# A planner-ordered graph-network stack: a 14th tile buffer, small softmax steps moved between engines, and the gate's difference by VectorE from PSUM

## The chip, the cores and the metric

The kernel runs on one core of one Trainium2 chip. The metric is the device time of one execution in microseconds (us). All arithmetic is float32.

## The reference

`x` is 64 graphs of 256 nodes with 128 features, and `adj` is one 256 x 256 matrix for all graphs. Four layers follow each other. Each normalises `x`, applies ReLU, runs a graph operator and adds its result to `x`.

```python
def layer0(h):                                   # gated recurrent unit, five steps
    for _ in range(5):
        m = einsum('nm,bmd->bnd', adj, h)        # m_in and m_out are the same
        av = concatenate([m, m]); u3 = h @ u3_w.T + u3_b
        z = sigmoid(av @ w3_w.T + w3_b + u3)
        r = sigmoid(av @ w4_w.T + w4_b + u3)
        hv = tanh(av @ w5_w.T + w5_b + (r * h @ u5_w.T + u5_b))
        h = (1 - z) * h + z * hv
    return h
def layer1(h):                                   # h, h@A and 2(h@A)@A - h, then Theta1, bias, relu
def layer2(h):                                   # (adj@h + h) @ weight + bias, each row over its norm
def layer3(x):                                   # pairwise attention; W is adj here
    pre = s1[:, :, None, :] + s2[:, None, :, :] + b_lin     # 256 x 256 x 256 for each graph
    e = einsum('bije,e->bij', where(pre >= 0, pre, 0.2 * pre), a) + adj
    return sigmoid(einsum('bij,bjf->bif', softmax(e, axis=2), x))
h = maximum(layernorm(x), 0); x = x + layerK(h)  # for K = 0, 1, 2, 3
```

Nearly all work is in `pre` of layer 3: 64 x 256 x 256 x 256 values of a sum, a kink and a weighted sum.

## The kernel before

The graphs are taken in 32 pairs. For each pair there are three kinds of work.

The **front** (`front`) does layers 0 to 2 and the projections of layer 3. It is one chain of about a hundred steps that hop between TensorE (PE), VectorE (DVE), ScalarE (ACT) and GpSimd (POOL). The first pair is done as two single graphs (`alone`). In each of the five steps of the recurrent unit ACT takes the tanh of the candidate out of a PSUM bank into `d` (L601), POOL subtracts the old state (`d - hT`, L605), and DVE multiplies by the gate (L608) and adds the state (L612). `norm` gives mean and variance by DVE (L463), then POOL the inverse root (`inverse_root`, L391 and L392), then DVE the product of minus mean and inverse root (L469), and then ACT applies both (L473).

The **tiles** are the body of layer 3. The kink is rewritten as a minimum (or a ReLU) of a column of `s1` and a row of `s2`, with the 256 hidden features in two halves of 128 partitions. A slot is four rows of two graphs, so one half of a slot is a tile of 128 x 2048 values. There are 2048 slots, so 4096 tiles. DVE makes tiles of the first half (L934, one instruction), ACT of the second (L946, eight), and POOL of either (L951, eight). PE scores a tile with four matmuls that sum over the features (`score`, L1010) into the score bank of that half of the pair. In a **joined** slot (a share of `SHARE`, here 3 in 10) DVE and POOL make one half each, an accumulating DMA that POOL issues (`add_pair`, L971) adds one tile to the other, and PE scores the sum once. The tiles lie in 13 SBUF buffers (`tiles`); a buffer is taken from the start of its making until PE has read it, or until the DMA has read it.

The **tail** (`tail`), twice in each pair, is the softmax and what follows: DVE adds a rank-one term to the scores (L806), POOL adds the broadcast rows `lin` (L818), DVE takes the row maximum (L822), ACT the exponential (L826), PE transposes and multiplies with `h3`, DVE takes the reciprocal (L846), ACT the tanh (L851), and POOL halves, adds 0.5 and adds the residual `x3` (L856, L857; in the very last tail these and the addition of `lin` are DVE's).

The order is written out ahead of time. A planner in the kernel keeps a clock for each engine, with a fixed cost for each operation (`ran`), and gives each engine in turn what is ready: steps of tails first, then steps of fronts (which may not run ahead of an even pace, `SPREAD`), then tiles. Tiles go to whichever of DVE, ACT and POOL is free. Each engine's instructions stay in that order on the chip (`in_order`); semaphores make them wait where the chip differs from the plan. SP's queue issues plain transfers: the inputs, `row` and `rows` (L745, L749) and the results (L860).

Of the kernel before, what the change touches and what calls it, by code (L numbers as in the profile page):

```python
# [21 lines left out]
MOST_POSITIVE = -MOST_NEGATIVE  # L22
PE, DVE, ACT, POOL = ENGINES = (mybir.EngineType.PE, mybir.EngineType.DVE, mybir.EngineType.Activation, mybir.EngineType.Pool)
SLOTS = 64
SHARE = (3, 10)
AHEAD_OF = 2
LOW = 1
ISSUE, ADDED, LANDED, SLACK = 0.65, 5.3, 6.6, 0.3

# [2 lines left out]
def kernel(  # L32
# [62 lines left out]
    banks = [psum.tile([P, NB * N], F32, name=f"bank{k}") for k in range(8)]  # L95


    clock = dict.fromkeys((PE, DVE, ACT, POOL), 0.0)
    queue = [0.0]
    SEEN = {PE: 0.25, DVE: 0.14, ACT: 0.18, POOL: 0.13}  # L100
# [21 lines left out]
    def by_feature(b, nb=NB):  # L122
        return b[:, 0:nb * N].rearrange("p (b n) -> p b n", b=nb)
# [31 lines left out]

    ident = const.tile([P, P], F32, name="ident")
    make_identity(nc, ident)
    place = work.tile([P, N], mybir.dt.int32, name="place", bufs=1)
# [19 lines left out]
    th_raw = const.tile([P, 5, D], F32, name="th_raw")  # L178
# [24 lines left out]
    gate_b = const.tile([P, 3], F32, name="gate_b")  # L203
    bz, br, bh = gate_b[:, 0:1], gate_b[:, 1:2], gate_b[:, 2:3]
    th = th_raw[:, 0:3, :]
# [9 lines left out]
    def first_constants():  # L215

        for c in range(NC):
            yield PE, 6.0, 1
            b = take()
            for k in range(NC):  # L220
                nc.tensor.transpose(b[0][:, k * P:(k + 1) * P], adj_n[:, k, c * P:(c + 1) * P], ident)
            t = ran(PE, 0.4, 6.0, b[1])
            yield DVE, t
            nc.vector.tensor_copy(adj_t[:, c, :], b[0][:, 0:N])
            t = ran(DVE, 0.35, t)
            spare.append([b[0], t])
# [28 lines left out]
        nc.vector.tensor_scalar(gate_b[:, 0:2], gate_b[:, 0:2], 0.5, None, op0=OP.mult)  # L255
        ran(DVE, 0.3)
        SET_UP.add("first")

# [196 lines left out]
    def norm(src, since, h):  # L455

        nb = src.shape[1]
        stats = work.tile([P, nb * NC, 3], F32, name="stats", bufs=4)
        mv = work.tile([P, nb * NC, 2], F32, name="mv", bufs=4)
        s, h = rows_of(src), rows_of(h)[:, :, 0:D]  # L460
        yield DVE, since
        for k in range(0, nb * NC, 2):
            nc.vector.bn_stats(stats[:, k:k + 2, :].rearrange("p k s -> p (k s)"), s[:, k:k + 2, :].rearrange("p k d -> p d k"))  # L463
        t = ran(DVE, STATS[nb], since)
        yield POOL, t
        inverse_root(mv[:, :, 1], stats[:, :, 2], 1.0 / D, OP.mult, LN_EPS, OP.add)
        t = ran(POOL, 1.45, t)
        yield DVE, t
        nc.vector.scalar_tensor_tensor(mv[:, :, 0], stats[:, :, 1], -1.0, mv[:, :, 1], op0=OP.mult, op1=OP.mult)  # L469
        t = ran(DVE, 0.1, t)  # L470
        yield ACT, t
        for k in range(nb * NC):
            nc.scalar.activation(h[:, k, :], s[:, k, :], AF.Relu, bias=mv[:, k, 0:1], scale=mv[:, k, 1:2])  # L473
        return ran(ACT, NORMED[nb], t)
# [5 lines left out]
    def front(p, batches):  # L480
# [31 lines left out]
        def seen(b):  # L512
            return by_feature(b[0], nb)
# [22 lines left out]
        for step in range(STEPS):  # L536
# [61 lines left out]
                t = ran(DVE, ELEMENTS[nb], t)  # L598
                spare.append([pv[0], t])
            else:  # L600
                nc.scalar.activation(d, seen(pv), AF.Tanh, bias=bh, scale=1.0)  # L601
                t = ran(ACT, TANH[nb], t)
                spare.append([pv[0], t])
                yield POOL, t
                nc.gpsimd.tensor_sub(d, d, hT)  # L605
                t = ran(POOL, 1.3, t)
            yield DVE, max(t, t_z)
            nc.vector.scalar_tensor_tensor(seen(pr), seen(pr), 1.0, d, op0=OP.add, op1=OP.mult)  # L608
            t = ran(DVE, ELEMENTS[nb], t, t_z)
            yield DVE, t  # L610
            hT_new = feature("hT", bufs=4)
            nc.vector.scalar_tensor_tensor(hT_new, seen(pr), 0.5, hT, op0=OP.mult, op1=OP.add)  # L612
            hT = hT_new
            t_hT = ran(DVE, ELEMENTS[nb])
            spare.append([pr[0], t_hT])
# [78 lines left out]
        t = ran(POOL, 1.35, t)  # L694

        yield DVE, t, 0, lambda: p < 2 or (p - 2, NC - 1) in TAILED
        x3 = kept("x3", [NC, D])
# [7 lines left out]
        h3 = kept("h3", [NC, D + 1])  # L705
        nc.gpsimd.memset(h3[:, :, :, D:D + 1], 2.0)
        t = yield from norm(x3, t, h3)
        yield PE, t, 1
        b = take()
        to_feature(b[0], h3)  # L710
        t = ran(PE, TURN[nb], t, b[1])
        yield ACT, t
        hT = kept("hT3", [N])
        nc.scalar.copy(hT, seen(b))
        t_hT = ran(ACT, COPY[nb], t)
        spare.append([b[0], t_hT])
        yield PE, t_hT, 1
        s2a = take()
        project(s2a[0], w2n[:, 0:P], hT)
# [13 lines left out]
        quarter = work.tile([P, P], F32, name="quarter", bufs=2)  # L733
# [4 lines left out]
        turned = work.tile([P, P], F32, name="turned", bufs=2)  # L738
        nc.vector.transpose(turned[:, 0:cols], quarter[:, 0:cols])
        s1o = kept("s1o", [NC])  # L740
        nc.vector.tensor_scalar(s1o.rearrange("p b c -> p (b c)"), turned[:, 2:cols:32], b_odd, None, op0=OP.add)
        ran(DVE, 0.65, t)
        row = dram.tile([2, NB * N], F32, name="row", bufs=4)
        for k in range(2):
            nc.sync.dma_start(row[k, 0:nb * N].rearrange("(q g i) -> g q i", g=4, i=32),  # L745
# [53 lines left out]
    def tail(u, pe, since):  # L799
# [3 lines left out]
        yield DVE, max(since, ops["t_lin"])  # L803
        sc = feat("sc", **SHORT)
        for k, (b, c) in enumerate(across(u)):
            nc.vector.scalar_tensor_tensor(sc[:, k, :], ops["s2o"][:, b, :], ops["s1o"][:, b, c:c + 1], pe[k], op0=OP.min, op1=OP.add)  # L806
        t = ran(DVE, 0.8, since, ops["t_lin"])
        used = banks_of.pop(u)
        spare.append([used, t])
        end = u == (NPAIR - 1, NC - 1)  # L810
        more = lin.to_broadcast([P, NB, N]) if ops["alone"] else lin
        if end:
            yield DVE, max(t, ops["t_lin"])
            nc.vector.tensor_add(sc, sc, more)
            t = ran(DVE, ELEMENTS[2], t, ops["t_lin"])
        else:
            yield POOL, max(t, ops["t_lin"])
            nc.gpsimd.tensor_add(sc, sc, more)  # L818
            t = ran(POOL, 1.3, t, ops["t_lin"])
        yield DVE, t  # L820
        nmx = work.tile([P, NB], F32, name="nmx")
        nc.vector.tensor_reduce(nmx, sc, AX.X, OP.max, negate=True)  # L822
# [40 lines left out]


    NSLOT = NPAIR * SLOTS
    tiles = [[relu_pool.tile([P, 4, NB, N], F32, name=f"rl{k}", bufs=1), 0.0] for k in range(13)]
    MOST = {DVE: 8, ACT: 3, POOL: 4}
    held = dict.fromkeys(MOST, 0)
    begun = {}
# [149 lines left out]


    CHAINS = {}
    STEPS_OF_FRONT, SPREAD, AHEAD = 109, 1.7, 2
    begun_fronts = [0]

    def begin(key, steps):
# [107 lines left out]
```

## Time and profile before

The median of three runs is 4924.24 us (4917.3 to 4930.92). The profiled execution took 4930.46 us, of which 4928.2 are the span from the first to the last instruction.

| engine | busy us | share of the span | its largest group | us of it |
|---|---|---|---|---|
| PE | 4768.4 | 97% | scoring, L1010 | 2211.3 and 1321.9 |
| DVE | 4713.3 | 96% | tiles, L934, 1817 of them | 4064.2 |
| POOL | 4670.5 | 95% | tiles, L951, 8144 instructions | 2966.0 and 874.8 |
| ACT | 4643.9 | 94% | tiles, L946, 10088 instructions | 4047.8 |
| DMA | | | joining, L971, 614 transfers of 1024 KB | 65.3% of 16 engines' span |

A group's line has the source line, the engine, the operation, its output and inputs by name, the shape and the count; behind the first bar stand the busy time of the group and the mean duration of one in ns; behind the second stand the engine's idle time just before these instructions and what ended it. Instructions of one engine overlap a little, so busy time over count can be less than the mean duration. A line of the view of waits has who waited for whom, the total in us, how often, and the longest.

### The profile page before, as it was taken

How to read it: one execution, taken by the hardware profiler on the slowest of the kernel's cores; microseconds unless marked ns; L12 is line 12 of the kernel's file. 1: busy time of each engine (PE TensorE's matmuls, PEld its weight loads, DVE VectorE, ACT ScalarE, POOL GpSimd, SP SyncE). 2: the span in 40 equal slices, each digit the busy share in tenths (PEclk: the TensorE clock that was granted, in tenths of full speed). 3: DMA queues.
4: the chain of work that ended last, by engine and by line, in shares of the span. 5: the costliest groups of instructions: out<-in, count | busy, mean ns of one | idle time of the engine just before them, and what ended most of it. 6: DMA issues, size and time to landing. Idle time of an engine off the chain costs nothing.

```text
span 4928.2 us, 134012 instructions
## 1 busy us (share of the span) xinstructions
PE 4768.4 (97%) x52471; PEld 1739.2 (35%) x52471; DVE 4713.3 (96%) x3389; ACT 4643.9 (94%) x12142; POOL 4670.5 (95%) x9473
## 2 busy tenths in 40 slices
PE   9999999999999999999999999999999999999987
PEld 4333333333333333333333333333333333333322
DVE  5999999999999999999999999999999999999998
ACT  6999999999999989999999999999999999999998
POOL 3999999999999999999999999999999999999997
PEclk9999999999999999999999999999999999999999
DMA  1666766767767666776776666777767767767677
GB/s 40 137 141 132 151 138 132 148 136 146 144 134 149 138 141 138 143 147 134 145 152 137 142 140 138 148 143 143 144 130 147 148 139 144 144 137 143 143 155 148
DMA packets 133540, 687.45 MB, mean 139 GB/s; under 512 B 15144, under 2 KB 50344, under 8 KB 54312
## 3 DMA queue, kind: packets, MB, share of 16 engines
q0 software_dynamic: 88416, 643.86, 65.3%
q1 hardware_dynamic: 43768, 35.01, 2.3%
q8 instruction: 410, 6.72, 0.5%
q14 instruction: 226, 1.85, 0.1%
q10 hardware_dynamic: 720, 0.00, 0.0%
HBM read 26.48 MB, written 8.52 MB: 7 GB/s over the span
## 4 chain that ended last, share of the span: by engine, by line
PE 31%; POOL 18%; DVE 12%; DMA 7%; ACT 6%; issue 4%; POOLq 0%; ACTq 0%; DVEq 0%
PE bank L1010 19%; POOL rl L951 14%; PE bank L397 11%; DVE rl L934 10%; DMA rl<-rl 7%; ACT rl L946 5%; POOL rl L971 2%; POOL d L605 1%; PE bank L428 1%; POOL mv L392 1%; DVE mv L469 0%; DVE hT L612 0%; PE bank L420 0%; DVE bank L608 0%; POOL sc L818 0%
## 5 line engine op out<-in xcount | busy, mean ns | idle before, releaser
L934 DVE TENSOR_TENSOR rl<-s1a,bank 128x2048 f32<-128x2048 f32 x1817 | 4064.2, 2277 | 100.3 <-DMA rl<-rl 59.2
L946 ACT ACTIVATE rl<-bank,s1b 128x256 f32<-128x256 f32 x10088 | 4047.8, 819 | 113.6 <-DMA rl<-rl 62.8
L951 POOL TENSOR_SCALAR rl<-s2n,s1b 128x256 f32<-128x256 f32 x6296 | 2966.0, 668 | 50.6 <-DMA rl<-rl 19.2
L1010 PE MATMUL bank<-rl,win_n 128*32 128x512 f32 x17768 | 2211.3, 596 | 56.0 <-DVE rl L934 28.0
L1010 PE MATMUL bank<-rl,win 128*32 128x512 f32 x10088 | 1321.9, 597 | 0.0
L1010 PEld LDWEIGHTS bank<-rl,win_n 128*32 128x32 f32 x17768 | 557.2, 110 | 1215.1 <-issue 981.7
L951 POOL TENSOR_SCALAR rl<-s2c,s1a 128x256 f32<-128x256 f32 x1848 | 874.8, 643 | 7.1 <-DMA rl<-rl 2.5
L971 POOL DMA_DIRECT2D rl<-rl x614 | 575.6, 944 | 29.0 <-DVE rl L934 14.8
L1010 PEld LDWEIGHTS bank<-rl,win 128*32 128x32 f32 x10088 | 323.4, 110 | 655.5 <-issue 532.1
L397 PE MATMUL bank<-mT,wts 128*32 128x512 f32 x2480 | 326.2, 594 | 1.6 <-ACT mT L521 1.3
L397 PE MATMUL bank<-adj_t,h 128*32 128x256 f32 x4960 | 300.5, 381 | 7.5 <-ACT h L623 6.4
L605 POOL TENSOR_TENSOR d<-d,hT 128x512 f32<-128x512 f32 x155 | 228.7, 1475 | 37.8 <-ACT d L601 37.8
L397 PEld LDWEIGHTS bank<-adj_t,h 128*32 128x32 f32 x4960 | 159.6, 110 | 178.7 <-issue 46.6
L473 ACT ACTIVATE h<-x,mv 128x128 f32<-128x128 f32 x376 | 176.2, 720 | 13.5 <-DVE mv L469 13.2
L565 ACT ACTIVATE bank<-bank,gate_b 128x512 f32<-128x512 f32 (+1 forms) x165 | 148.5, 900 | 19.4 <-PE bank L397 14.3
L397 PE MATMUL bank<-mT,w 128*32 128x512 f32 x1240 | 163.3, 593 | 3.6 <-ACT bank L565 3.6
L397 PE MATMUL bank<-rh,u5t 128*32 128x512 f32 x1240 | 163.2, 592 | 2.3 <-DVE rh L569 2.3
L588 ACT ACTIVATE bank<-bank,gate_b 128x512 f32<-128x512 f32 (+1 forms) x165 | 154.0, 934 | 9.5 <-PE bank L397 9.4
L397 PE MATMUL bank<-hT,wts 128*32 128x512 f32 x1240 | 162.6, 593 | 0.0
L521 ACT COPY mT<-bank 128x512 f32<-128x512 f32 x155 | 137.1, 885 | 26.8 <-PE bank L397 24.8
L428 PE MATMUL bank<-ident,hT 128*128 128x128 f32 x620 | 101.7, 287 | 57.4 <-DVE hT L612 54.4
L601 ACT ACTIVATE d<-bank,gate_b 128x512 f32<-128x512 f32 x155 | 149.3, 963 | 3.6 <-PE bank L397 3.6
(204 smaller groups left out, 3494.8 us busy)
## 6 DMA issues: line engine op xcount, KB each, us to landing
rl<-rl POOLq DMA_DIRECT2D x614, 1024.0 KB, 7.8
rows<-row SPq DMA_DIRECT2D x31, 512.0 KB
xin<-in_x_dram SPq DMA_DIRECT2D x64, 128.0 KB
out_dram<-o SPq DMA_DIRECT2D x64, 128.0 KB
row<-quarter SPq DMA_DIRECT2D x62, 2.0 KB
rows<-row SPq DMA_DIRECT2D x2, 256.0 KB
w_raw<-in_L_gnn_w_w_dram SPq DMA_DIRECT2D x3, 128.0 KB
th_raw<-in_L_gnn_Theta_dram SPq DMA_DIRECT2D x1, 320.0 KB
```

The source lines that it names most:

```text
L397: nc.tensor.matmul(o[g:g + 32], w[:, g:g + 32], t, start=start, stop=stop, skip_group_check=True)
L428: nc.tensor.transpose(pt[:, b, c, :], ht[:, b, c * P:(c + 1) * P], ident)
L473: nc.scalar.activation(h[:, k, :], s[:, k, :], AF.Relu, bias=mv[:, k, 0:1], scale=mv[:, k, 1:2])
L565: nc.scalar.activation(seen(r), seen(pr), AF.Tanh, bias=br, scale=0.5)
L588: nc.scalar.activation(seen(pr), seen(pr), AF.Tanh, bias=bz, scale=0.5)
L601: nc.scalar.activation(d, seen(pv), AF.Tanh, bias=bh, scale=1.0)
L605: nc.gpsimd.tensor_sub(d, d, hT)
L934: nc.vector.tensor_tensor(t, rows.to_broadcast(whole), ops["s2a"].unsqueeze(1).to_broadcast(whole), op=OP.min)
L946: nc.scalar.activation(t[:, g, b, :], other(ops["s2p"][0], b), AF.Relu, bias=rows[:, g, b], scale=-1.0)
L951: nc.gpsimd.tensor_scalar(t[:, part, b, :], other(ops["s2n" if k else "s2c"], b), rows[:, part, b], MOST_NEGATIVE, op0=OP.min, op1=OP.max)
L971: nc.gpsimd.dma_start(out=t.rearrange("p g b n -> p (g b n)"), in_=z.rearrange("p g b n -> p (g b n)"), accum_op=OP.add)
L1010: nc.tensor.matmul(pe[g * 32:(g + 1) * 32, :], w[:, 31 - r:63 - r], flat(t[:, g]), start=False, stop=(left[u] == 0), skip_group_check=True)
```

## The change

- **Tile buffers.** There are 14 in place of 13. The space comes from scratch data of the set-up (`place`, `th_raw`), which now lies in the first tile buffer, and from `quarter` and `turned`, which have one buffer each in place of two, and from `hT3`, which now shares the four `hT` buffers.
- **Joined slots.** The share is 1 in 3, but none of the last 96 slots (`ALONE`) is joined.
- **Recurrent unit.** ACT leaves minus the tanh in its PSUM bank, DVE adds the state to it from there (new L608), and the sign is taken back in the last operation (-0.5). POOL has no part in it.
- **Norm.** DVE negates the mean by a `tensor_reduce` right behind the statistics (new L469), and POOL multiplies by the inverse root (new L473).
- **Tail.** DVE writes the rank-one sum back into the score bank (new L812) and adds `lin` from there (new L816). ACT leaves the tanh in PSUM, and one DVE instruction halves it and adds the residual (new L853). POOL adds the 0.5 to `x3` once for each pair (new L713).
- **s1o.** The addition of a bias to 128 x 4 values is ACT's in place of DVE's.
- **Pace.** `SPREAD` is 1.8 in place of 1.7. Some planner costs follow the edits.

The planner deals the tiles out anew. In the order of the changed kernel DVE makes 1751 tiles (1817 before), ACT 1254 (1261) and POOL 1091 (1018). There are 650 joined slots (614), so PE scores 3446 tiles (3482). The last projection of a pair's front stands 19 to 23 scored tiles ahead of the first score of that pair (28 to 31 before), and 9 ahead for the last pair (25).

```diff
-SHARE = (3, 10)
+SHARE = (1, 3)
+ALONE = 96
...
+    tiles = [[relu_pool.tile([P, 4, NB, N], F32, name=f"rl{k}", bufs=1), 0.0] for k in range(14)]
+    scratch = tiles[0][0].rearrange("p g b n -> p (g b n)")
...
-        t = ran(DVE, STATS[nb], since)
+        nc.vector.tensor_reduce(mv[:, :, 0], stats[:, :, 1:2], AX.X, OP.add, negate=True)
+        t = ran(DVE, STATS[nb], since) + 0.1
         yield POOL, t
         inverse_root(mv[:, :, 1], stats[:, :, 2], 1.0 / D, OP.mult, LN_EPS, OP.add)
-        t = ran(POOL, 1.45, t)
-        yield DVE, t
-        nc.vector.scalar_tensor_tensor(mv[:, :, 0], stats[:, :, 1], -1.0, mv[:, :, 1], op0=OP.mult, op1=OP.mult)
-        t = ran(DVE, 0.1, t)
+        nc.gpsimd.tensor_mul(mv[:, :, 0], mv[:, :, 0], mv[:, :, 1])
+        t = ran(POOL, 1.55, t)
         yield ACT, t
...
-                nc.scalar.activation(d, seen(pv), AF.Tanh, bias=bh, scale=1.0)
+                nc.scalar.activation(seen(pv), seen(pv), AF.Tanh, bias=bh_n, scale=-1.0)
                 t = ran(ACT, TANH[nb], t)
+                yield DVE, t
+                nc.vector.tensor_add(d, seen(pv), hT)
+                t = ran(DVE, ELEMENTS[nb], t)
                 spare.append([pv[0], t])
-                yield POOL, t
-                nc.gpsimd.tensor_sub(d, d, hT)
-                t = ran(POOL, 1.3, t)
...
-            nc.vector.scalar_tensor_tensor(hT_new, seen(pr), 0.5, hT, op0=OP.mult, op1=OP.add)
+            nc.vector.scalar_tensor_tensor(hT_new, seen(pr), 0.5 if alone else -0.5, hT, op0=OP.mult, op1=OP.add)
...
+        yield POOL, t
+        nc.gpsimd.tensor_scalar(x3, x3, 0.5, None, op0=OP.add)
+        ran(POOL, 0.45 if alone else 0.7, t)
...
+        yield ACT, t_s
         s1o = kept("s1o", [NC])
-        nc.vector.tensor_scalar(s1o.rearrange("p b c -> p (b c)"), turned[:, 2:cols:32], b_odd, None, op0=OP.add)
-        ran(DVE, 0.65, t)
+        nc.scalar.activation(s1o.rearrange("p b c -> p (b c)"), turned[:, 2:cols:32], AF.Identity, bias=b_odd, scale=1.0)
+        ran(ACT, 0.2, t_s)
...
-            nc.vector.scalar_tensor_tensor(sc[:, k, :], ops["s2o"][:, b, :], ops["s1o"][:, b, c:c + 1], pe[k], op0=OP.min, op1=OP.add)
+            nc.vector.scalar_tensor_tensor(pe[k], ops["s2o"][:, b, :], ops["s1o"][:, b, c:c + 1], pe[k], op0=OP.min, op1=OP.add)
         t = ran(DVE, 0.8, since, ops["t_lin"])
+        yield DVE, t
         used = banks_of.pop(u)
+        nc.vector.tensor_add(sc, by_feature(used), lin.to_broadcast([P, NB, N]) if ops["alone"] else lin)
+        t = ran(DVE, ELEMENTS[2], t)
         spare.append([used, t])
...
-            yield POOL, max(t, ops["t_lin"])
-            nc.gpsimd.tensor_add(sc, sc, more)
-            t = ran(POOL, 1.3, t, ops["t_lin"])
...
+        for k in range(NB):
+            nc.scalar.activation(po[:, k, 0:D], po[:, k, 0:D], AF.Tanh, scale=rs[:, k:k + 1])
+        t = ran(ACT, 0.5, t, t_s)
+        yield DVE, t
         o = work.tile([P, NB, D], F32, name="o")
-        for k in range(NB):
-            nc.scalar.activation(o[:, k, :], po[:, k, 0:D], AF.Tanh, scale=rs[:, k:k + 1])
-        t = ran(ACT, 0.5, t, t_s)
+        nc.vector.scalar_tensor_tensor(o, po[:, :, 0:D], 0.5, x3[:, 0] if ops["alone"] else x3[:, :, u[1], :], op0=OP.mult, op1=OP.add)
+        t = ran(DVE, 0.36, t)
         spare.append([bank[0], t])
-        yield DVE if end else POOL, t
-        e = nc.vector if end else nc.gpsimd
-        e.tensor_scalar(o, o, 0.5, 0.5, op0=OP.mult, op1=OP.add)
-        e.tensor_add(o, o, x3[:, 0] if ops["alone"] else x3[:, :, u[1], :])
-        ran(DVE, 0.6, t) if end else ran(POOL, 1.2, t)
...
-    JOINED = [n for n in range(NSLOT) if (n + 1) * SHARE[0] // SHARE[1] > n * SHARE[0] // SHARE[1]]
+    JOINED = [n for n in range(NSLOT - ALONE) if (n + 1) * SHARE[0] // SHARE[1] > n * SHARE[0] // SHARE[1]]
...
-    STEPS_OF_FRONT, SPREAD, AHEAD = 109, 1.7, 2
+    STEPS_OF_FRONT, SPREAD, AHEAD = 109, 1.8, 2
```

More of the change, by code (lines that the diff above doesn't have):

```diff
@@ L157 @@
     make_identity(nc, ident)
-    place = work.tile([P, N], mybir.dt.int32, name="place", bufs=1)
+    place = scratch[:, 0:N].bitcast(mybir.dt.int32)
     nc.gpsimd.iota(place, pattern=[[1, N]], base=0, channel_multiplier=0)
@@ L177 @@
         nc.scalar.dma_start(braw[:, k:k + 1], v.rearrange("(p o) -> p o", o=1))
-    th_raw = const.tile([P, 5, D], F32, name="th_raw")
+    th_raw = scratch[:, N:N + 5 * D].rearrange("p (k o) -> p k o", k=5)
     nc.sync.dma_start(th_raw, theta.rearrange("(k f) o -> f k o", f=P))
@@ L202 @@
     u5t = const.tile([P, P], F32, name="u5t")
-    gate_b = const.tile([P, 3], F32, name="gate_b")
-    bz, br, bh = gate_b[:, 0:1], gate_b[:, 1:2], gate_b[:, 2:3]
-    th = th_raw[:, 0:3, :]
+    gate_b = const.tile([P, 4], F32, name="gate_b")
+    bz, br, bh, bh_n = (gate_b[:, k:k + 1] for k in range(4))
+    th = const.tile([P, 3, D], F32, name="th")
     win = const.tile([P, 63], F32, name="win")
@@ L255, in first_constants @@
         nc.vector.tensor_scalar(gate_b[:, 0:2], gate_b[:, 0:2], 0.5, None, op0=OP.mult)
+        nc.vector.tensor_scalar(bh_n, bh, -1.0, None, op0=OP.mult)
         ran(DVE, 0.3)
@@ L693, in front @@
         inverse_root(rn, rn, MOST_POSITIVE, OP.min, NORM_EPS * NORM_EPS, OP.max)
-        t = ran(POOL, 1.35, t)
+        t = ran(POOL, 1.35, t) + 0.1
         yield DVE, t, 0, lambda: p < 2 or (p - 2, NC - 1) in TAILED
@@ L712, in front @@
         yield ACT, t
[L713 to L716, printed above, removed]
+        hT, t_hT = copied("hT", b, t, bufs=4)
         yield PE, t_hT, 1
@@ L732, in front @@
         yield ACT, t
-        quarter = work.tile([P, P], F32, name="quarter", bufs=2)
+        quarter = work.tile([P, P], F32, name="quarter", bufs=1)
         nc.scalar.copy(quarter[:, 0:cols], b[0][:, 0:cols])
@@ L737, in front @@
         yield DVE, t
-        turned = work.tile([P, P], F32, name="turned", bufs=2)
+        turned = work.tile([P, P], F32, name="turned", bufs=1)
         nc.vector.transpose(turned[:, 0:cols], quarter[:, 0:cols])
+        t_s = ran(DVE, 0.2, t)
+        yield ACT, t_s
         s1o = kept("s1o", [NC])
-        nc.vector.tensor_scalar(s1o.rearrange("p b c -> p (b c)"), turned[:, 2:cols:32], b_odd, None, op0=OP.add)
-        ran(DVE, 0.65, t)
+        nc.scalar.activation(s1o.rearrange("p b c -> p (b c)"), turned[:, 2:cols:32], AF.Identity, bias=b_odd, scale=1.0)
+        ran(ACT, 0.2, t_s)
         row = dram.tile([2, NB * N], F32, name="row", bufs=4)
@@ L805, in tail @@
         for k, (b, c) in enumerate(across(u)):
-            nc.vector.scalar_tensor_tensor(sc[:, k, :], ops["s2o"][:, b, :], ops["s1o"][:, b, c:c + 1], pe[k], op0=OP.min, op1=OP.add)
+            nc.vector.scalar_tensor_tensor(pe[k], ops["s2o"][:, b, :], ops["s1o"][:, b, c:c + 1], pe[k], op0=OP.min, op1=OP.add)
         t = ran(DVE, 0.8, since, ops["t_lin"])
+        yield DVE, t
         used = banks_of.pop(u)
+        nc.vector.tensor_add(sc, by_feature(used), lin.to_broadcast([P, NB, N]) if ops["alone"] else lin)
+        t = ran(DVE, ELEMENTS[2], t)
         spare.append([used, t])
[L810 to L816, printed above, removed]
-            yield POOL, max(t, ops["t_lin"])
-            nc.gpsimd.tensor_add(sc, sc, more)
-            t = ran(POOL, 1.3, t, ops["t_lin"])
         yield DVE, t
@@ L865 @@
     NSLOT = NPAIR * SLOTS
-    tiles = [[relu_pool.tile([P, 4, NB, N], F32, name=f"rl{k}", bufs=1), 0.0] for k in range(13)]
     MOST = {DVE: 8, ACT: 3, POOL: 4}
```

## The prediction

> **What bounds the kernel now.** I read the busy totals first, then the groups by shape, then the waits, then the last 40 us. The page's first part:
>
> ```profile
> PE 4768.4 (97%) x52471; PEld 1739.2 (35%) x52471; DVE 4713.3 (96%) x3389; ACT 4643.9 (94%) x12142; POOL 4670.5 (95%) x9473
> ```
>
> No engine has more than 6% to spare, so there is no single bound. DVE, ACT and POOL share one pool of tiles and are dealt them as they come free, so work taken from one of the three is worth about a third of itself at the end. PE must score what they make. Its busy time counts a lone tile at 1.04 us, but the chain of work has "PE bank L1010 x96" in 10.30 us, which is 12 tiles at 0.858 us. So a tile less on PE saves 0.858 us.
>
> The groups by shape give the prices:
>
> ```profile
> L934 DVE TENSOR_TENSOR rl<-s1a,bank 128x2048 f32<-128x2048 f32 x1817 | 4064.2, 2277 | 100.3 <-DMA rl<-rl 59.2 <-PE bank L1010 34.0 <-POOL rl L951 2.7
> L605 POOL TENSOR_TENSOR d<-d,hT 128x512 f32<-128x512 f32 x155 | 228.7, 1475 | 37.8 <-ACT d L601 37.8
> L818 POOL TENSOR_TENSOR sc<-sc,rows 128x512 f32<-128x512 f32 x63 | 87.4, 1387 | 4.1 <-DVE sc L806 4.0
> L469 DVE SCALAR_TENSOR_TENSOR mv<-stats,mv 128x4 f32<-128x4 f32 x124 | 61.1, 493 | 13.4 <-POOL mv L392 12.7
> L690 DVE TENSOR_REDUCE rn<-sq 128x4 f32<-128x512 f32 x31 | 21.0, 678 | 2.2 <-ACT sq L686 2.2
> L628 DVE TENSOR_TENSOR x<-xin,bank 128x512 f32<-128x512 f32 x31 | 21.0, 677 | 0.0
> ```
>
> Busy time over count is the price of a tile: DVE 2.237 us, ACT 8 x 0.4013 = 3.21 us (4047.8 / 10088), POOL 8 x 0.4716 = 3.77 us (3840.8 / 8144).
>
> The waits say that the makers' idle time is partly want of a free tile buffer:
>
> ```profile
> ACT rl L946 <- DMA rl<-rl: 62.8, 43, 3.7
> DVE rl L934 <- DMA rl<-rl: 59.2, 46, 3.3
> ACT rl L946 <- PE bank L1010: 44.3, 62, 3.5
> DVE rl L934 <- PE bank L1010: 34.0, 62, 2.4
> PE bank L1010 <- DMA rl<-rl: 27.1, 23, 3.7
> POOL rl L951 <- DMA rl<-rl: 21.7, 18, 4.7
> DVE bank L608 <- POOL d L605: 17.6, 26, 2.0
> DVE mv L469 <- POOL mv L392: 15.6, 25, 1.5
> DVE nmx L822 <- POOL sc L818: 7.6, 17, 1.1
> ```
>
> A maker that waits for the DMA or for PE waits for a buffer to come back: 93 us on DVE, 107 on ACT, 34 on POOL (with 12.2 behind PE), 78 each on average. The last three lines are DVE standing behind small POOL steps.
>
> **The change, part by part.**
>
> *DVE.* It makes 66 tiles fewer: -66 x 2.237 = -147.6. The gate's difference comes over: 155 x 0.677 = +104.9 (L628 has that form: one operand in PSUM, one in SBUF). So does the addition of `lin`: 64 x 0.677 - 0.7 = +42.6 (one was DVE's already). The residual is 64 instructions of 128x256 at 0.432 (L806: 55.3 / 128), less 0.7 that DVE spent in the last tail: +26.9. `s1o` leaves: -20.5. The norm's product leaves, -62.6 with the single graphs', and 132 reductions to four values come in. The trace has no reduction that small; L690 takes 0.678 for 512 values, of which 508 / 2048 of a tile's 2.237 (0.55) is streaming, so about 0.15. Bounds 0.13 (the shortest L469 is 0.144) and 0.49. I take 0.15: +19.8. Sum: -36.5.
>
> [...] L469 by itself:
>
> ```profile
> L469 DVE SCALAR_TENSOR_TENSOR mv<-stats,mv x132: 144/166/6596, 5.0 to 4727.1; 128x4 f32<-128x4 f32 x124, 128x2 f32<-128x2 f32 x8
> ```
>
> Median 0.166, but mean 0.493 and longest 6.6 us: it is sometimes held. [...] L469 has two SBUF inputs. L690 never shows it (mean equals a clean instruction), so by the row the new reduction is not held. If it were held like L469, it would cost 132 x 0.49 = 65 and DVE would gain nothing (+8 instead of -36). I take the row.
>
> [...] 677 ns with a PSUM operand (L628) stands against 678 from SBUF alone (L690). I take nothing.
>
> *ACT.* 56 instructions less: -56 x 0.4013 = -22.5. `s1o` comes in 33 times; no activation this small is in the trace. Bounds 0.1 and 0.69 (L734, 128x128, takes 0.69); L473 adds up to 0.47 each for 128 columns with queues full, so I take 0.35: +11.5. Its tanh goes to PSUM instead of SBUF: 965 ns (L588, into a bank) against 963 (L601, into `d`), nothing. Sum: -11.
>
> *POOL.* 584 instructions more: +275.4. 36 more join issues at 0.9375 (575.6 / 614): +33.8. Leaving: L605 -228.7, L818 -87.4, L856 -25.8, L857 -46.2. New: 132 products of four values. Bounds 0.13 (its memset of four, L706) and 1.03 (the power of four, L392); the one-operand step on four takes 0.195 (L391), and I take 0.2: +26.4. `x3 + 0.5`: 31 of 128x512 at about 0.75 (L856 takes 0.41 for half): +24. Sum: -28.5.
>
> *Three makers:* (-36.5 - 11 - 28.5) / 3 = **-25**. *PE:* 36 tiles less, -31, so it doesn't hold that up. With the unknown costs at their dear ends (reduction +45, `s1o` +11, product +110, sum 166 / 3) it becomes +30; at their cheap ends -32.
>
> *Waits.* DVE's three waits for POOL (40.8) and POOL's waits for ACT and DVE in the same steps (37.8 + 6.2 + 4.0, of which one of 22.1 is in the first pair) lose their cause. What comes instead: DVE waits for ACT's tanh before the difference and before the residual, with DVE's tiles queued behind it and PE behind those; and ACT waits for a 0.3 us transpose before `s1o`. I count 20 on DVE and 13 on POOL as saved, a third for the whole: **-11** (bounds 0 and -25). SP's store of `o` now follows DVE instead of POOL; its queue stands in order, but nothing reads the result.
>
> *The 14th buffer.* A tile lives 13 x 4800 / 4096 = 15.2 us, so one more buffer gives 1.17 us of slack against waits of 1.3 us mean. But joins get denser: 614 in 4800 us now, 650 in about 4606 afterwards (96 slots without, 192 tiles at about 1 us, are left out). Each holds two tiles for 7.8 us, its median to landing; 650 x 2 x 7.8 / 4870 = 2.08 tiles against 1.94, more if landing slows. If 0.6 of a buffer is left, waits with an exponential spread fall by 42%, 33 us of 78. The plan itself was made with the extra tile and will spend some of it, so I take a third: **-11** (bounds 0 and -33). PE's own waits for tiles (27.1 + 28.0) shrink with it.
>
> *The end.*
>
> ```profile
> 4906.36 0.86 POOL L971 DMA_DIRECT2D rl<-rl  x1 [3.96 <-DVE rl L934]
> 4910.76 3.64 PE L1010 MATMUL bank<-rl,win_n 128*32 128x512 f32 x16 [3.65 <-DMA rl<-rl]
> 4916.98 0.87 DVE L806 SCALAR_TENSOR_TENSOR sc<-rows,s1o,bank 128x256 f32<-128x256 f32 x2 [8.96 <-PE bank L1010]
> ```
>
> The last tile is made at 4908.0, and the last tail starts at 4917.0, because two joins have to land. Without joins there, a last score of under 2 us remains: **-7**. The 29 joins taken out of the last 96 slots put 29 x 0.858 = 25 us back on PE, which is 85% busy there (17 of 20 us in the stretches from 4800 on), so they are hidden; without that cover they would cost 25.
>
> *At nothing:* the scratch in tile buffer 0 (read before the first tile is made, over 80 us in), single `quarter` and `turned` (next used a pair, 150 us, later), shared `hT` buffers, and `SPREAD` (a front still ends 19 tiles ahead; the cover is gone once that is below the 13 or 14 tiles that makers run ahead, and it is once, at the last pair, with 9: a few us).
>
> *Sum:* -25 - 11 - 11 - 7 = -54, so a span of 4928.2 - 54 = 4874 and a profiled execution of 4876. That execution (4930.46) is 6.2 us above the median of its kernel (4924.24), so the median comes to **4870 us**, 1.1% less.
>
> **The rivals.**
>
> *Work only.* Tile and chain waits come back elsewhere, since PE and the makers run as tightly against each other as before: -25 and part of the end, about 4895 to 4900. For it: the waits are spread over 200 short ones. Against: their named causes go.
>
> *No change.* The products of four values on POOL and the reductions are near their dear ends (+30 in place of -25) and cancel the saved waits: 4924. For it: L392 takes 1.03 us for four values. Against: L391 does four in 0.195.
>
> *Slower: joins land later.* The joining queue fills 65.3% of the engines' span, 5.24 us for each join. Spacing goes from 7.8 to 7.1 us, 67% to 74% full. If landing goes from 7.8 to above 11 us, the two tiles that each join holds eat the whole 14th buffer (650 x 2 x 11 / 4870 = 2.94 against 1.94). By the same exponential, at 13.3 us the waits grow by 58 us and decide for slower; at 14 us it is about +39, 4963. For it: the longest landing today is 14.5 us. Against: the median is 7.8 and the shortest 6.7, so the queue seldom stacks up.
>
> *The buffer is worth its full slack:* -25 - 25 - 33 - 7 = -90, 4834.
>
> **How the numbers follow.** The forecast (4840 to 4890) 0.58, the full slack 0.07, work only 0.15, no change 0.10, slower 0.10. A measurement of this kernel tells about 0.3% (15 us) from no change: faster 0.80, same 0.10, slower 0.10. The range of 4828 to 4922 leaves out the slower case, half of no change, and little below.
>
> **What would show it.** Right: L605, L818, L856 and L857 gone from POOL; DVE busy near 4677, POOL near 4642, ACT near 4633, PE near 4737; the new reduction at 0.15 us and the new product at 0.2; a maker's waits for buffers near 65 us in place of 78; tail start within 3 us of the last tile. Wrong: a product or reduction of four values at 0.5 us or more, a median landing above 9 us, DVE idle behind ACT's tanh for over 40 us, or a maker's waits above 80.

## The result: 1.1% faster, and the profile after

The changed kernel takes 4869.23 us (median of four runs, 4868.41 to 4870.96) against 4923.82 us. The ratio is 0.9889 with a 95% interval of 0.9872 to 0.9906. The forecast was 4870 us. The sum was right, but most of its terms were not, as the experiments show.

First the busy totals, as the first part of the page of the changed kernel has them (its span is 4869.2 us):

```profile
PE 4729.6 (97%) x52183; PEld 1750.1 (36%) x52183; DVE 4666.6 (96%) x3571; ACT 4630.5 (95%) x12119; POOL 4693.2 (96%) x9914
```

PE's 38.8 us less and DVE's 46.7 less go the forecast's way, and ACT's 13.4 less fits. POOL was forecast 28 us lighter and is 23 us heavier, while the span is 59 us shorter.

The groups by shape of the changed kernel, in the columns of before:

```profile
L930 DVE TENSOR_TENSOR rl<-s1a,bank 128x2048 f32<-128x2048 f32 x1751 | 3921.6, 2279 | 105.7 <-DMA rl<-rl 75.4 <-PE bank L1006 13.8 <-POOL rl L947 13.2
L812 DVE SCALAR_TENSOR_TENSOR bank<-rows,s1o,bank 128x256 f32<-128x256 f32 x128 | 62.4, 487 | 16.8 <-PE bank L1006 14.1 <-issue 0.3
L608 DVE TENSOR_TENSOR d<-bank,hT 128x512 f32<-128x512 f32 x155 | 106.0, 684 | 5.2 <-ACT bank L605 5.1
L816 DVE TENSOR_TENSOR sc<-bank,rows 128x512 f32<-128x512 f32 x64 | 43.7, 682 | 0.0
L853 DVE SCALAR_TENSOR_TENSOR o<-bank,x 128x256 f32<-128x256 f32 x64 | 26.8, 418 | 2.4 <-ACT bank L849 2.4
L469 DVE TENSOR_REDUCE mv<-stats 128x4 f32<-128x4 f32 x124 | 19.7, 159 | 4.2
L473 POOL TENSOR_TENSOR mv<-mv 128x4 f32<-128x4 f32 x124 | 24.6, 199 | 9.7
L713 POOL TENSOR_SCALAR x<-x 128x512 f32<-128x512 f32 x31 | 46.7, 1507 | 2.4
```

What came over to DVE costs what the old rows said: 684 and 682 ns against 677 for one operand in PSUM, 418 against 432 for the half width. One cost of PSUM was not entered: the rank-one sum, now written into the bank (L812), is busy for 62.4 us where it was 55.3 (L806), and 55.5 again in the experiment below that writes it to SBUF. The reduction takes 159 ns (150 forecast), the product on POOL 199 (200 forecast). The surprise is L713: 1507 ns, twice the 750 of the forecast.

The waits of the changed kernel:

```profile
DVE rl L930 <- DMA rl<-rl: 75.4, 60, 3.8
ACT rl L942 <- DMA rl<-rl: 48.1, 28, 4.4
ACT rl L942 <- PE bank L1006: 19.5, 23, 2.2
DVE rl L930 <- PE bank L1006: 13.8, 18, 1.9
POOL rl L947 <- DMA rl<-rl: 9.3, 14, 2.2
ACT h L477 <- POOL mv L473: 48.5, 45, 2.9
DVE d L608 <- ACT bank L605: 5.1, 7, 2.2
```

The waits for a tile buffer are 89 us on DVE, 68 on ACT and 11 on POOL (with 1.8 behind PE): 56 on average, where they were 78. DVE's 41 us behind POOL's small steps are gone, and only 5 have come behind ACT's tanh. In exchange ACT waits 48.5 us for POOL's product in the norm, where before it waited 27.9 for DVE's:

```profile
ACT h L473 <- DVE mv L469: 27.9, 12, 5.1
```

The median landing of a join is 8.4 us (7.8 before).

Last, the end, from the timeline (start, duration, engine, line):

```profile
4851.04 5.89 ACT L942 ACTIVATE rl<-bank,s1b 128x256 f32<-128x256 f32 x14
4851.31 2.28 DVE L930 TENSOR_TENSOR rl<-s1a,bank 128x2048 f32<-128x2048 f32 x1
4858.06 1.01 DVE L812 SCALAR_TENSOR_TENSOR bank<-rows,s1o,bank 128x256 f32<-128x256 f32 x2 [4.47 <-PE bank L1006]
```

The last tile is ACT's, done at 4856.9, and the last tail starts 1.1 us later. Before, it started 9.0 us after the last tile.

### The profile page after: what moved, and what is told of

Same layout as the page of the kernel before. It is cut to its first block, busy times and chain, and to the rows that moved or that the text cites. A ratio compares the mean times of both kernels' runs of the same rounds, so it can differ in the third digit from the quotient of the medians.

```text
span 4869.2 us, 134117 instructions
## 1 busy us (share of the span) xinstructions
PE 4729.6 (97%) x52183; PEld 1750.1 (36%) x52183; DVE 4666.6 (96%) x3571; ACT 4630.5 (95%) x12119; POOL 4693.2 (96%) x9914
## 4 chain that ended last, share of the span: by engine, by line
PE 48%; POOL 16%; DVE 15%; DMA 10%; ACT 6%; issue 4%; POOLq 0%; DVEq 0%; SPq 0%; ACTq 0%
PE bank L1006 29%; PE bank L402 17%; POOL rl L947 13%; DVE rl L930 12%; DMA rl<-rl 10%; ACT rl L942 4%; POOL rl L967 1%; PE bank L433 1%; PE bank L425 1%; POOL mv L397 1%; DVE hT L616 1%; DVE bank L612 0%; ACT h L477 0%; DVE d L608 0%; DVE rh L573 0%
## 5 line engine op out<-in xcount | busy, mean ns | idle before, releaser
L930 DVE TENSOR_TENSOR rl<-s1a,bank 128x2048 f32<-128x2048 f32 x1751 | 3921.6, 2279 | 105.7 <-DMA rl<-rl 75.4
L942 ACT ACTIVATE rl<-bank,s1b 128x256 f32<-128x256 f32 x10032 | 3946.2, 691 | 75.4 <-DMA rl<-rl 48.1
L947 POOL TENSOR_SCALAR rl<-s2n,s1b 128x256 f32<-128x256 f32 x6352 | 3043.6, 789 | 28.4 <-DMA rl<-rl 8.6
L947 POOL TENSOR_SCALAR rl<-s2c,s1a 128x256 f32<-128x256 f32 x2376 | 1155.4, 747 | 5.0 <-DMA rl<-rl 0.7
L967 POOL DMA_DIRECT2D rl<-rl x650 | 689.4, 1077 | 9.4 <-PE bank L1006 2.2
L477 ACT ACTIVATE h<-x,mv 128x128 f32<-128x128 f32 x376 | 162.7, 572 | 41.3 <-POOL mv L473 41.2
L569 ACT ACTIVATE bank<-bank,gate_b 128x512 f32<-128x512 f32 (+1 forms) x165 | 138.5, 840 | 20.9 <-PE bank L402 13.6
L402 PEld LDWEIGHTS bank<-mT,wts 128*32 128x32 f32 x2480 | 81.6, 110 | 186.0 <-issue 149.6
L397 POOL TENSOR_TENSOR mv<-mv,minus_half 128x4 f32<-128x4 f32 (+1 forms) x132 | 134.0, 1015 | 11.0
L525 ACT COPY mT<-bank 128x512 f32<-128x512 f32 x155 | 119.5, 771 | 26.2 <-PE bank L402 26.0
L592 ACT ACTIVATE bank<-bank,gate_b 128x512 f32<-128x512 f32 (+1 forms) x165 | 134.1, 813 | 10.2 <-PE bank L402 9.9
```

The source lines that it names most:

```text
L397: nc.gpsimd.tensor_tensor(t, t, minus_half[:, 0:t.shape[1]], op=OP.pow)
L402: nc.tensor.matmul(o[g:g + 32], w[:, g:g + 32], t, start=start, stop=stop, skip_group_check=True)
L525: nc.scalar.copy(c, seen(bank))
L569: nc.scalar.activation(seen(r), seen(pr), AF.Tanh, bias=br, scale=0.5)
L592: nc.scalar.activation(seen(pr), seen(pr), AF.Tanh, bias=bz, scale=0.5)
L930: nc.vector.tensor_tensor(t, rows.to_broadcast(whole), ops["s2a"].unsqueeze(1).to_broadcast(whole), op=OP.min)
```

## The experiments

Each kernel is set against the kernel before on the same chip, since chips and hours differ by up to 0.3% (its median was 4923.82 to 4939.25 us in the four groups). Where I give a difference to the changed kernel in us, it is the difference of the two ratios times 4924, or the difference of times where both ran on one chip in one group (the old share, the gate and the tail, set against the second measurement of the changed kernel at the end). An interval of a ratio is about 0.17% to each side, so 8 us, and that of a difference of two ratios about 12 us. Except for the two experiments "in the same order", the planner deals all tiles out anew in each; what a new deal is worth by itself was not measured and is part of each difference.

**Without the 14th buffer.**

```diff
-... for k in range(14)]
+... for k in range(13)]
```

> The changed kernel with 13 tile buffers instead of 14, all else kept. My account gives the 14th buffer 11 us (bounds 0 and 33), so 4880 us against 4869. Rival 1, the buffer is worth its full slack: 4902. Rival 2, it is only eaten by the denser joins and 13 would do: 4869 to 4872. The makers' waits for a buffer (56 us each on average in the changed kernel's trace) should go up by as much as the time does.

Measured: 4899.85 us, ratio 0.9934 (0.9917 to 0.9950), so 22 us slower than the changed kernel by the ratios (30 by the times, which are of two chips). Its waits:

```profile
DVE rl L930 <- DMA rl<-rl: 96.0, 61, 4.7
ACT rl L942 <- DMA rl<-rl: 56.7, 40, 4.2
DVE rl L930 <- PE bank L1006: 31.8, 48, 3.0
POOL rl L947 <- DMA rl<-rl: 21.9, 24, 2.6
```

With 12.2 on ACT and 11.8 on POOL behind PE, waits for a buffer are 230 us, 77 for each maker, 21 more than with 14. The time goes up by as much, and by twice what I had put down. Rival 2 has fallen; the value lies between my 11 and the full slack's 33.

**The 14th buffer alone**, put into the kernel before with what makes room for it (scratch in tile 0, single `quarter` and `turned`, shared `hT`):

> The kernel before with one part of the change: the 14th tile buffer, with what makes room for it, all else as before (614 joins). My account gave the buffer 11 us: 4913. Taking it away from the changed kernel cost 30 us. If it is worth as much here: 4895. If the 30 us came from the denser joins, which hold more tiles: 4905 to 4913. Rival, no use without less load on PE: 4920 to 4926.

Measured: 4917.54 us where the kernel before took 4939.25 in that group, ratio 0.9949 (0.9932 to 0.9966): 22 us faster by the medians, 25 by the ratio. So the buffer is worth 22 to 25 us with either share of joins; the denser joins are not what makes it valuable. In its trace, that of the fastest of its five executions, a maker waits 54 us for buffers on average, 24 less than before.

**The old share of joins.**

```diff
-SHARE = (1, 3)
+SHARE = (3, 10)
```

> The changed kernel with the old share of joined slots, 3 in 10 (585 joins, PE scores 3511 tiles instead of 3446). If PE's load matters as much as the makers', 65 scorings more at 0.858 us cost up to 56 us, against 65 issues less on POOL at 0.70 us from start to start, a third of which is 15: between 4854 and 4925, by my account (PE does not hold the makers up) at the lower end, 4860. Rival, PE sets the time: 4900 to 4925.

Measured: 4907.54 us against 4869.56 for the changed kernel in the same group, 38 us slower; ratio 0.9963 (0.9948 to 0.9978). My account said 9 us faster. Here are the stretches from 100 to 4500 us of the kernel before, the changed kernel and this one, in that order (stretch, its length, then the busy time of PE, weight loads, DVE, ACT and POOL, the clock, the DMA share and GB/s):

```profile
100.00:4500.00 4400.00, 4300.11 (x47390) 1565.50 (x47386) 4259.07 (x2987) 4195.47 (x10957) 4254.21 (x8619) 1.00 0.69 141
```

```profile
100.00:4500.00 4400.00, 4284.32 (x47290) 1565.23 (x47286) 4263.26 (x3189) 4222.82 (x11044) 4322.61 (x9101) 1.00 0.77 158
```

```profile
100.00:4500.00 4400.00, 4297.55 (x47478) 1563.14 (x47474) 4267.32 (x3182) 4103.99 (x10698) 4302.05 (x9118) 1.00 0.69 142
```

With the old share PE is as full as before (4298 of 4400), POOL is full as well (4302), and ACT stands still for 296 us (177 in the changed kernel). In the whole run it waits 62 us for PE to give a buffer back (19.5 in the changed kernel), but also 81 for joins to land (48). The loads say more: with 65 joins fewer POOL has 65 issues less and fewer tiles are held by joins, and only PE has more to do, 4775.6 us busy in place of 4729.6, 46 more for a time that is 38 longer. So PE did hold the makers up, unless the new deal is to blame. The step "PE: 36 tiles less, -31, so it doesn't hold that up" has fallen.

**The share alone**, in the kernel before (1 in 3, none in the last 96 slots; 13 buffers, gate and tail as before):

> The kernel before with one part of the change: joined slots 1 in 3 and none in the last 96 slots. Undoing the share in the changed kernel cost 38 us, so PE's load did hold the makers up, against my account. New theory: in the body PE and POOL bind together, so a denser join helps only where POOL has room. Here POOL has 36 issues more at 0.70 us and keeps the gate, the tail's sums and the 13 buffers, so a part of the 38 us shows, 4900 to 4915. Rival 1, PE alone binds: all of it, 4880 to 4890. Rival 2, work is worth a third of itself on any maker, as in my prediction: 4917 to 4925 (25 us more on POOL, 7 us gained at the end).

Measured: 4924.06 us against 4939.25, ratio 0.9966 (0.9953 to 0.9979), 15 us faster by the medians and 17 by the ratio: a part of the 38, between rivals 1 and 2, as the new theory has it. In this form it comes to 4924 x 0.9966 = 4907, inside its 4900 to 4915. It takes as many scorings out of the body, and the joins out of the end as well, and still gives less than half of the 38. That PE's relief counts in full only where POOL has been relieved too is a reading that fits; the missing 14th buffer, or DVE's waits for POOL, would do as well, and the three were not separated.

**Joins up to the last slot.**

```diff
-ALONE = 96
+ALONE = 0
```

> The changed kernel with joined slots up to the last slot (ALONE 0, 682 joins). My account gives the end 7 us: 4876, with the last tail starting about 9 us behind the last tile, where it starts 4.5 us behind DVE's last tile in the changed kernel. Rival: with 32 scorings less, PE's load sets the time and the end doesn't matter, 4855 to 4869.

Measured: 4909.45 us, ratio 0.9954 (0.9939 to 0.9969), 32 us slower than the changed kernel by the ratios (40 by the times on two chips), where I gave it 7. The makers' orders are those of the changed kernel up to about 4650 us, so the loss lies behind that. A part of it is the end: the last tail starts at 4894.75, 8.8 us behind DVE's last tile (4.5 in the changed kernel). But the larger part is earlier. Here are a stretch of 20 us in the last but one pair and the waits between 4700 and 4800 us:

```profile
4730.00:4750.00 20.00, 13.56 (x116) 4.00 (x120) 11.85 (x7) 12.06 (x33) 11.29 (x21) 0.97 0.84 170
```

```profile
POOL rl L947 <- ACT s1b L782: 14.6, 1, 14.6
DVE bank L812 <- PE bank L1006: 10.9, 1, 10.9
ACT s2n L765 <- PE bank L402: 9.6, 1, 9.6
```

All makers fall to 60% or less: the last pair's front isn't ready (L782 is its projection). In the order its last projection stands 0 scored tiles ahead of its first use, where the changed kernel has 9.

**The same with the old pace of the fronts.**

```diff
-ALONE = 96
+ALONE = 0
...
-    STEPS_OF_FRONT, SPREAD, AHEAD = 109, 1.8, 2
+    STEPS_OF_FRONT, SPREAD, AHEAD = 109, 1.7, 2
```

> The changed kernel with joins up to the last slot, as in the second experiment (4909), and the old pace of the fronts (1.7). In the second experiment all makers dropped to 60% around 4730 to 4760 us while POOL waited 14.6 us for the last pair's projection, and that pair's front ended 0 scored tiles ahead of its first use; with 1.7 it ends 21 ahead. Theory: the late front is what cost most of the 40 us, so the stall goes and the time is 4880 to 4892, the end's two landings staying. Rival: joins at the end cost it by themselves, 4900 to 4910.

Measured: ratio 0.9983 (0.9975 to 0.9992), 4933.44 us against 4939.25. The stall is gone: between 4700 and 4800 us DVE is busy for 98 us here and for 87 in the experiment before. The third row is the changed kernel:

```profile
4700.00:4800.00 100.00, 85.21 (x780) 25.13 (x780) 97.96 (x60) 97.99 (x268) 99.30 (x213) 0.95 0.84 172
```

```profile
4700.00:4800.00 100.00, 85.22 (x732) 25.38 (x731) 86.89 (x56) 87.13 (x237) 84.73 (x178) 0.95 0.73 151
```

```profile
4700.00:4800.00 100.00, 100.00 (x938) 41.21 (x934) 95.89 (x55) 99.39 (x275) 99.50 (x221) 1.00 0.03 10
```

But the time is not better, so my theory that the late front explains most of the loss has fallen. I followed the first instruction of each score bank in the three traces. From the fifth last bank to the last tail the changed kernel takes 330 us, joins to the end 357, and joins to the end with the old pace 346. So, as far as single traces tell, 11 of the 27 us lost there went with the late front, and 16 stay with the joins. Why they stay was not separated: in the rows of this experiment and of the changed kernel the makers are busy for 96 to 100 us of 100, but PE for 85 with the joins and 100 without, and its granted clock is 0.95 with them and 1.00 without.

By the ratios the old pace is 14 us slower than the experiment before, though its end is shorter, so it loses elsewhere. From the third bank to the seventh last its trace takes 4153 us against 4140 with 1.8. But the changed kernel, whose order is the same as that of the 4140 up to there, takes 4131 on its own chip, and the trace of the old pace is that of the fastest of its twelve executions, 20 us below their median. So what the pace is worth in the body is not shown; the pace alone was not run.

**The gate's difference back on POOL.**

```diff
-                nc.scalar.activation(seen(pv), seen(pv), AF.Tanh, bias=bh_n, scale=-1.0)
+                nc.scalar.activation(d, seen(pv), AF.Tanh, bias=bh, scale=1.0)
...
-                nc.vector.tensor_add(d, seen(pv), hT)
...
+                nc.gpsimd.tensor_sub(d, d, hT)
...
-            nc.vector.scalar_tensor_tensor(hT_new, seen(pr), 0.5 if alone else -0.5, hT, op0=OP.mult, op1=OP.add)
+            nc.vector.scalar_tensor_tensor(hT_new, seen(pr), 0.5, hT, op0=OP.mult, op1=OP.add)
```

> The changed kernel with the gated unit's difference back on POOL, tanh into SBUF, as before. POOL takes 155 times 1.33 us more, DVE 155 times 0.61 less (from start to start in the traces). By my account a third of the difference, 37 us, and some 5 us of DVE waiting for POOL: 4906 to 4911. Rival, the move was neutral because DVE is as loaded as POOL: 4869 to 4880.

Measured: 4891.10 us against 4869.56, 21.5 us slower; ratio 0.9930 (0.9916 to 0.9945). The move pays, but less than a third of its work, which would be 37. DVE waits for POOL again, more than in the kernel before (17.6):

```profile
DVE bank L612 <- POOL d L609: 66.2, 66, 2.8
```

**The tail's sums back on POOL** (and no 0.5 added to `x3`).

```diff
-        nc.vector.tensor_add(sc, by_feature(used), lin.to_broadcast([P, NB, N]) if ops["alone"] else lin)
...
+            nc.gpsimd.tensor_add(sc, sc, more)
...
-        nc.vector.scalar_tensor_tensor(o, po[:, :, 0:D], 0.5, x3[:, 0] if ops["alone"] else x3[:, :, u[1], :], op0=OP.mult, op1=OP.add)
...
+        e.tensor_scalar(o, o, 0.5, 0.5, op0=OP.mult, op1=OP.add)
+        e.tensor_add(o, o, x3[:, 0] if ops["alone"] else x3[:, :, u[1], :])
```

> The changed kernel with the tail's later sums back on POOL (the addition of lin, and half of the tanh plus 0.5 plus x3), and without the addition of 0.5 to x3. POOL takes 63 times 2.55 us more and 49 us less, DVE 66 us less. A third of the sum, 15 us, and some 4 us of waits of DVE for POOL: 4884 to 4889. Rival, the 1.5 us of the x3 line on POOL ate the gain and the old tail is as good: 4865 to 4873.

Measured: 4880.41 us, 11 us slower; ratio 0.9909 (0.9894 to 0.9924). It lies between the two theories. The wait that the move removes is there again, at 32.5 us (7.6 in the kernel before):

```profile
DVE nmx L825 <- POOL sc L821: 32.5, 34, 2.0
```

**A reduction against two SBUF inputs**, in the same order.

```diff
-        nc.vector.tensor_reduce(mv[:, :, 0], stats[:, :, 1:2], AX.X, OP.add, negate=True)
+        nc.vector.tensor_mul(mv[:, :, 0], stats[:, :, 1], minus_one[:, 0:nb * NC])
```

> The changed kernel with the norm's reduction to four values replaced by a product of the mean with a constant tile of -1, so that VectorE has two SBUF inputs at that place; same order. Theory: an instruction with two SBUF inputs is held while POOL works, as the old L469 was (0.166 median, 0.493 mean, 6.6 us longest), so its 132 instances cost 43 us more on DVE than the reduction's 159 ns, and the time is 14 us longer, 4883. Rival: the old line was held by something else (a wait on POOL's power that the trace shows as its duration), since the new product waits for no result of POOL; then it takes 0.16 us and the time is 4869.

Measured: the product takes 572 ns in the mean, though it waits for nothing of POOL's; the reduction in its place takes 154 to 161 ns in every instance.

```profile
L471 DVE TENSOR_TENSOR mv<-stats,minus_one 128x4 f32<-128x4 f32 x124 | 71.0, 572 | 4.3
```

```profile
L471 DVE TENSOR_TENSOR mv<-stats,minus_one x132: 160/311/2678, 3.9 to 4715.1; 128x4 f32<-128x4 f32 x124, 128x2 f32<-128x2 f32 x8
```

The trace agrees with the theory: the product with two SBUF inputs is held (572 ns in the mean, 2678 at most) where POOL is busy for 4325 of the 4400 us from 100 to 4500, and the old line's hold was no hidden wait. In the kernel before, the seven L469 that ran with no POOL instruction beside them took 161 ns at most, the other 125 took 493 in the mean. DVE is busy 48 us more here. The time is 4883.61 us, ratio 0.9902 (0.9888 to 0.9917): 6 us slower by the ratios, 14 by the times on two chips. Both are less than 48, and neither is clear of noise; a third of the 48 would be 16.

**L713 as two operations**, in the same order of all instructions.

```diff
-        nc.gpsimd.tensor_scalar(x3, x3, 0.5, None, op0=OP.add)
+        nc.gpsimd.tensor_scalar(x3, x3, 1.0, 0.5, op0=OP.mult, op1=OP.add)
```

> The changed kernel with the addition of 0.5 to x3 on POOL written as two operations, times 1.0 and plus 0.5, in the same instruction and the same place; the order of all instructions is the same. In the changed kernel this line takes 1.507 us for 128x512, twice what I had put down from a line of two operations (0.41 us for 128x256). Theory: POOL runs the two-operation form of this instruction faster, so the line falls to about 0.75 us, 23 us of POOL in all, and the time falls by a third of it, to about 4861. Rival 1: the form makes no difference, 1.5 us and 4869. Rival 2: the line gets faster but the order was planned without it, and the time stays within 3 us of 4869.

Measured: 4852.77 us, ratio 0.9839 (0.9825 to 0.9854). The line:

```profile
L713 POOL TENSOR_SCALAR x<-x 128x512 f32<-128x512 f32 x31 | 19.4, 625 | 2.4
```

1507 ns became 625, which is 27 us of POOL in all, and the time fell by 25 us by the ratios, with 12 us to each side (16 by the times on two chips, of which this one is the slower). So at a fixed order POOL's time counted for more than a third, which would be 9, and perhaps one for one. In the body of the changed kernel POOL is busy for 4323 of 4400 us, and in a fixed order nobody takes its work.

**A 15th buffer** (short-lived tiles 8 instead of 12) with L713 as two operations:

```diff
-... for k in range(14)]
+... for k in range(15)]
...
-    SHORT = dict(tag="short", bufs=12)
+    SHORT = dict(tag="short", bufs=8)
```

> A version that may beat both kernels: the changed kernel with the x3 line in two operations (4853 us by itself) and a 15th tile buffer, whose room comes from the short-lived tiles (8 buffers in place of 12). If a buffer more is still worth half of the 30 us that the 14th was: 4838. If the fewer short buffers make the fronts wait: 4853 to 4875, with waits of ACT or DVE in the front that the changed kernel does not have.

Measured: ratio 0.9868 (0.9852 to 0.9885), 4874.34 us against 4939.25. That beats the changed kernel by 10 us, about the interval, and loses 14 to L713 alone. PE waits less for landings (32.3 us with L713 alone, 14.6 here), but ACT waits twice as long in the norm (50.1 there):

```profile
ACT h L477 <- POOL mv L473: 102.2, 68, 3.8
PE bank L1006 <- DMA rl<-rl: 14.6, 14, 3.1
```

A maker waits 44 us for buffers on average, 45 with L713 alone, so the 15th buffer took no waits away. Whether the fewer short buffers or the newly dealt order causes the loss was not separated.

**The changed kernel again**, as a measure for the group:

> The changed kernel itself, to stand beside the next three on the same chip. It took 4869.2 us (ratio to before 0.9889); the kernel before was 8 us slower in the first group of experiments than in the first measurement, so ratios are compared, and this run says how far they hold: 0.987 to 0.991.

Measured: 4869.56 us, ratio 0.9888 (0.9871 to 0.9904).

The best version is the changed kernel with L713 in two operations: 1.6% faster than the kernel before, 0.5% faster than the change.

## Why the prediction was right, and where it was wrong

**Work of the makers, -25: wrong, -12.5 by busy time.** DVE (-46.7 instead of -36.5) and ACT (-13.4 instead of -11) were fair; POOL (+22.7 instead of -28.5) had the wrong sign. Two steps failed. The term of 0.75 us for `x3 + 0.5`, worked out from L856, took the price of a two-operation line for a one-operation line; it was 1.507, 23 us more. And the tile and issue prices were busy time over count. The groups' busy times overlap, above all an issue and the tile behind it, so such prices don't add up to POOL's total. The timeline of POOL in the changed kernel shows it:

```profile
1999.78 3.68 POOL L947 TENSOR_SCALAR rl<-s2n,s1b 128x256 f32<-128x256 f32 x8
2003.34 0.96 POOL L967 DMA_DIRECT2D rl<-rl  x1
2003.97 7.38 POOL L947 TENSOR_SCALAR rl<-s2n,s1b 128x256 f32<-128x256 f32 x16
2011.11 1.07 POOL L967 DMA_DIRECT2D rl<-rl  x1
```

From start to start a tile is 3.56 here and an issue 0.63 (0.457 x 8 = 3.65 and 0.70 over both traces). At these prices POOL's sum is +267 +25 for tiles and issues, -206 for the gate, -161 for the tail, +36 for the products and +49 for L713: +10. That has the right sign; the total rose by 22.7.

**A third for each maker, PE not in the way: wrong.** The old share cost 38 us, where this account had it 9 us faster. PE's 65 scorings less in the body were the costliest part to take out, and I had entered them as nothing. POOL's 27 us came back at more than a third, DVE's 48 counted for 6 to 14, and for ACT nothing was run. So PE and POOL seem to bind ahead of DVE. The gate's move, (206 - 95) / 3 = 37 by the rule of a third, gave 21.5; the tail's, 15, gave 11.

**The 14th buffer, -11: right mechanism, too small.** It is worth 22 (taken out) to 25 (put in), inside the bounds of 0 and 33. Makers' waits for buffers fell to 56 us where I had named 65. One reading in it was wrong: 1.3 us is the mean of the waits for the DMA alone, while the 78 us also hold those behind PE. Over all 250 of these waits the mean is 0.94, and the same exponential then gives 53% in place of 42%, 41 us in place of 33.

**Chain waits, -11: seen in the trace, not measured alone.** DVE's 41 us behind POOL went, and 5 came behind the tanh and 2 before the residual, so more was saved there than the 20 that I had counted. That ACT would wait 21 us more for POOL in the norm I had not entered.

**The end, -7: right at the end itself** (1.1 us from the last tile to the tail, 9.0 before), but the joins kept out of the last 96 slots are worth 32 us. A part is that the last front is not pushed late (11 us by the traces); why the joins there cost the rest stays open. Entering `SPREAD` at nothing, with a few us for the last pair, missed that margin: with joins to the end it falls from 9 tiles to 0.

**Held instruction and PSUM operand: right.** The reduction was not held (161 ns at most), the product of two SBUF inputs was (2678 at most), and an input in PSUM cost nothing extra (684 and 682 ns against 692 for the same form with both inputs in SBUF, L814 of the very last tail before). An output there did, 7 us in all (L812, 62.4 us against 55.3), which I had not entered.

So the time came out within 1 us for a different mix, and that it came so close is luck. The makers' work gave half of its term, and PE's relief and the buffer, both entered too low, seem to have made up for it; how much each gave in the whole can't be told, since the single effects don't add up. Taken out one by one, buffer, share, last slots, gate and tail cost 22 + 38 + 32 + 21.5 + 11 = 124 us, more than twice the 54.6 that all give together. The buffer is worth the same put in alone (22 to 25); the share with the last slots, put in alone, gives 15 to 17.

## What to carry to other kernels

In this kernel, with four engines over 95% busy, a share of its work did not tell what a change was worth. Put a change in alone and take it out of the whole: the two differed by a factor of two here (38 us and 15 to 17 for the denser joins), and relief on the engine that takes in what the others make was worth more than any relief of theirs that was run (38 us with PE's 65 scorings, against 25 for POOL's 27 us and 6 to 14 for DVE's 48). Take prices from start to start in the timeline where instructions overlap (an issue of a join 0.70 us, against 0.94 by busy time over count), and only from a row of the same form, number of operations included (L713: 1507 ns with one, 625 with two). A buffer more in a shared pool was worth about what the waits for it shrank by, averaged over those who wait (22 us for 21, and 22 to 25 for 24).

## What was not expected of the hardware

POOL ran the addition of 0.5 in place slower as one operation than as two (times 1.0, plus 0.5): 1507 against 625 ns for 128x512 float32, and 862 against 402 for 128x256, in the same place of the same order. VectorE's products of 128x4 values with two SBUF inputs took up to 2.7 us where POOL was busy for 4325 of 4400 us (6.6 in the kernel before, at 4254), against 0.16 for the reduction. A single tensor input did not spare a line such durations: the addition of a column to 128x4 values, both in SBUF (L741 of the kernel before), took from 229 to 4372 ns.
